# Graph layer with residual and norm on one core: constants of the compares in PSUM, picks on four banks, more chunks gathered, codes of edges by bf16 products

## The chip, the core and the metric

One core of a Trainium2 chip runs the whole layer in one launch. Its engines work side by side, each in the order of its own queue: TensorE (PE, matmuls; PEld are its weight loads), VectorE (DVE), ScalarE (ACT), GpSimd (POOL, which here issues the indirect gathers) and SyncE (SP, which issues the other transfers). They meet at semaphores. The metric is device time in microseconds, the median of three runs.

## What is computed

12,500 nodes with 128 features, 400,000 edges sorted by destination, two types of edge.

```python
Xs = X[src]
m_data = Xs @ W_data.T + b_data
m_ctrl = Xs @ W_control.T + b_control
msg = where((edge_types == 0)[:, None], m_data, m_ctrl)
agg = segment_sum(msg, dst, num_segments=N)
out = relu(agg + X @ W_self.T + b_self)
x = layernorm(x + out)
```

The kernel sums the rows of X by destination and type first and multiplies by the weights afterwards, which gives the same sums with far fewer products. A row of X is kept as three bf16 parts of 128 columns that add up to the float32 value, so a row has 384 columns.

## The kernel before

**Chunks and groups.** 128 edges are a chunk; 3125 chunks make 25 groups of 125 (`GC`). Since edges are sorted, a chunk's destinations lie in a narrow window of rows. A group has five pairs of windows: five chunks that are *gathered* (`PB`), then 20 that are *picked* (`EC`). A pair's picked part is called a set. `sets(g)` says how many sets a group has: five where `g % EACH == 0`, else four, and then the last window's 25 chunks are all gathered. With `EACH = 3` that is 109 sets and 945 gathered chunks.

**Gathered chunks.** POOL issues one indirect DMA a chunk, which fetches 128 rows of 384 bf16 from DRAM into `msg` (`fetch`, L887; 18 buffers). PE multiplies its three parts by a 0/1 matrix `psel` (L803 through `add_rows`), and DVE adds the result to the accumulator (L876). `paced` ties each gather to a matmul: there are eleven such places in a set, and a gather is due 14 chunks before its use (`AHEAD`).

**Picked chunks.** X itself lies in SBUF (`x3`). A set's 2560 edges are sorted into 98 cells by source block with 32 slots each: DVE builds one-hot matrices and running counts (`give_slots`, L541 to L713), and the result comes back by way of DRAM as `pick`, which DVE turns into 0/1 (L790). A cell's rows are then picked by PE: `pick` (128x32) times a block of `x3` (384 columns), four cells side by side in the four 32-row strips of a PSUM bank (L997). ACT casts the bank to bf16 (`emsg`, L1011), and PE multiplies by the 0/1 matrix `esel` (L803). Edges of overfull cells are fetched by a second kind of indirect DMA, `both` (L963), once for two sets.

**Turns.** A set goes in five turns of five cell rows (`bounds` 0, 5, 10, 15, 19, 24; `unit`, `rows`). A turn uses a tile of two banks and one of three (`got2`, `got3`): 5 x 4 matmuls of 384 columns. With the bank of `side` and the two of `sums` all eight banks are taken. In the fourth turn the 25th cell row is picked in halves.

**Compares.** `select` (L541) makes every one-hot matrix on DVE by comparing a constant row (`cell_col0/1`, `rank_col`, `code_col`, `near_col`, bf16 in SBUF) with codes that are repeated in pairs. A set has five: `O` (2000 columns), `rm` (640) and `esel` (1720, 1548, 1032); a window of gathered chunks has `psel` (1200, always for 25 chunks).

**Codes.** `prep(g)` turns a group's sources, destinations and types into codes: DVE subtracts the window's first row (`rel`, L498), marks the type (`kind`, L499) and adds type times width (`code`, L500 and L501); PE transposes three float32 tiles (L508); ACT writes them out.

**Order.** Work is written down set by set: `merged` sorts the pieces of a set by a position between 0 and 1, `in_turn` chains DVE's own steps in a list with such positions, and the recording layer then orders each engine's queue by its own model of times. When a group's last window is done, its sums are passed on and finished (`pass_on`, `finish`).

Of the kernel before, what the change touches and what calls it, by code (L numbers as in the profile page):

```python
# [8 lines left out]
FP = mybir.dt.float32  # L9
BF = mybir.dt.bfloat16  # L10
# [9 lines left out]
P = 128  # L20
D = 128
# [13 lines left out]
EACH = 3  # L35
# [173 lines left out]
def short_path(ctx, tc, const, ident, eps, wT, brow, bad, x, src, dst, etype, ws, bs, out):  # L209
# [10 lines left out]
    psg = ctx.enter_context(tc.tile_pool(name="psg", bufs=1, space=PSUM))  # L220

# [12 lines left out]
    def sets(g):  # L234

        return NE if g % EACH == 0 else NE - 1

# [115 lines left out]
    near_col = table(2 * PW, 0, "near_col")  # L353
    ident_b = keep.tile([P, P], BF, name="ident_b")
# [41 lines left out]
    bounds_of, from_of, pick_first = row_tables(nc, keep, tmp)  # L396
    least = tmp.tile([1, NG, NWIN], FP, name="least")
# [81 lines left out]
    def prep(g):  # L479
# [3 lines left out]
        width = bounds_of[:GC, v, 0:1]  # L483
        sf = pre.tile([GC, P], FP, name="sf", bufs=1)
        rel = pre.tile([GC, 2, P], BF, name="rel", bufs=1)
        code = pre.tile([GC, 2, P], FP, name="code_r", bufs=1)
        kind = pre.tile([GC, P], FP, name="kind_r", bufs=1)
# [7 lines left out]
        def rows():  # L495
            near = near_of(g, d)
            for k in range(2):
                nc.vector.tensor_scalar(rel[:, k], d, near[k], None, op0=OP.subtract)  # L498
            nc.vector.tensor_single_scalar(kind, t, 0.0, op=OP.not_equal)  # L499
            nc.vector.scalar_tensor_tensor(code[:, 1], kind, width, rel[:, 1], op0=OP.mult, op1=OP.add)  # L500
            nc.vector.scalar_tensor_tensor(code[:, 0], kind, float(PW), rel[:, 0], op0=OP.mult, op1=OP.add)  # L501
            for j, op in enumerate((OP.max, OP.min)):
                nc.vector.tensor_tensor(worst[:GC, v, j], worst[:GC, v, j], rel, op=op)
# [297 lines left out]
    def add_rows(out, msg, sel, start, stop):  # L801
        for j in range(3):
            last = nc.tensor.matmul(  # L803
                out, msg[:, j * D:(j + 1) * D], sel, start=(start and j == 0), stop=stop, skip_group_check=True
            )
        return last
# [116 lines left out]
    def gathered(g, i):  # L923
# [9 lines left out]
        def chunk(c):  # L933
# [9 lines left out]
            add_rows(rows, s["msg"], sel, c == 0, c == n - 1)  # L943
# [24 lines left out]
    def picked(w, tiled, ending, before):  # L968
# [26 lines left out]
        def pick(ps, q, a0=0, a1=4, last=None):  # L995
            for a in range(a0, a1):
                last = behind(last, lambda: nc.tensor.matmul(  # L997
                    ps[CAP * a:CAP * (a + 1), :], slots[w]["pick"][:, a * NQ + q, :],
                    x3[:, 4 * q + a - a0].rearrange("p j d -> p (j d)"), start=True, stop=True, skip_group_check=True,
                ))  # L1000
            return last

        def rows(q, n, room, half=False):
            ps = psg.tile([P, room, 512], FP, name=f"got{room}")
            msg = two.tile([P, room, 3 * D], BF, name=f"emsg{room}")
            for k in range(n):
                last = pick(ps[:, k, :3 * D], q + k, last=last if k else None)
                s["msg"][q + k] = msg[:, k, :]
            if half:
                last = pick(ps[:, n, :3 * D], NQ - 1, lead, lead + 2, last)  # L1010
            s["out"] = nc.scalar.copy(msg[:, :n], ps[:, :n, :3 * D])  # L1011
            if half:
                nc.scalar.copy(s["msg"][NQ - 1][half_rows, :], ps[half_rows, n, :3 * D])
            return last
# [8 lines left out]
        def unit(t):  # L1023

            if t == 3:
                assert not spare
                if "both" in slots[w]:
                    slots[w]["last"] = two.tile([P, 3 * D], BF, name="last", bufs=1)
                s["msg"][NQ - 1] = slots[w]["last"]
            paced(w + (t + 0.5) / turns, rows(bounds[t], 2, 2))  # L1030
            if t == 1 and w > 0 and w % 2 == 0:
                spare.append(lambda: spare_rows(w))
            gate = rows(bounds[t] + 2, bounds[t + 1] - bounds[t] - 2, 3, t == 3)
# [13 lines left out]
            if t == 2:  # L1047
                paced(w + (t + 1) / turns, gates[-1])
# [203 lines left out]
    for w in range(pairs):  # L1252
# [63 lines left out]
        for p in closed.pop(w, []):  # L1316
            gp, ip = divmod(p, NE)
            if ip == NE - 1:
                rest.append(lambda gp=gp: pass_on(gp))
                if gp < NG - 1:  # L1320
                    rest += finish(gp, range(4))
                if gp + 2 < NG:
                    rest.append(lambda gp=gp: begin_acc(gp + 2))
# [143 lines left out]
```

## Time and profile before

| what | us |
|---|---|
| median of three runs | 1671.41 |
| lowest, highest | 1670.22, 1672.55 |
| the profiled execution | 1674.53 |
| its span, first to last instruction | 1672.8 |

How the core's time divides over the run (busy in tenths, 40 equal slices):

```profile
PE   1699999999999999999999999999999999999988
DVE  9799998999999999999999999999999999999983
ACT  7677776777777778667777778677777777777764
POOL 1377777767787787888787887878787787888881
PEclk9899999999999999999999999999999999999999
```

A slice is 42 us. The first two are the setup, in which X is split into its three parts; from there on the sets follow each other evenly, and the last slice is the end of the last group. In the body DVE and PE are busy nearly throughout, ACT and POOL about three quarters. [...] The chain of waits, followed back from the end, runs mostly over DVE and PE:

```profile
DVE 57%; PE 25%; issue 7%; ACT 6%; DMA 3%; DVEq 2%; SPq 0%; POOL 0%; ACTq 0%; POOLq 0%
```

### The profile page before, as it was taken

Reading aid. Unit: us, or ns where it says so; the run is one execution under the profiler, and the core shown is the slowest. Engines: PE = TensorE matmul, PEld = TensorE weight load, DVE = VectorE, ACT = ScalarE, POOL = GpSimd, SP = SyncE. Lnnn points to the kernel's source line nnn. Section 1 sums busy time; section 2 is a strip of 40 time slices with the busy share of each in tenths; the row PEclk is TensorE's granted clock in tenths of the full one; section 3 lists DMA queues with packets and bytes.
Section 4 is the critical chain, followed back from the end, with each engine's and each line's share of the span. In section 5 each row is a group of like instructions: output and inputs, shape, how many; then the busy total and the mean of one; then the engine's idle time right before and its main releaser. Section 6 shows DMA issues by size and latency. Waiting matters only on the chain.

```text
span 1672.8 us, 67687 instructions
## 1 busy us (share of the span) xinstructions
PE 1542.5 (92%) x27966; PEld 1218.8 (73%) x27966; DVE 1566.8 (94%) x4078; ACT 1221.0 (73%) x2056; POOL 1244.2 (74%) x1022
## 2 busy tenths in 40 slices
PE   1699999999999999999999999999999999999988
PEld 0477777777777777777777777777777777777766
DVE  9799998999999999999999999999999999999983
ACT  7677776777777778667777778677777777777764
POOL 1377777767787787888787887878787787888881
PEclk9899999999999999999999999999999999999999
DMA  7944444554455454444454445454545444554541
GB/s 223 283 142 136 143 139 134 154 148 141 142 156 145 147 155 133 150 140 143 149 156 139 148 142 152 139 159 135 158 124 164 147 144 131 157 152 126 151 124 33
DMA packets 147605, 246.05 MB, mean 147 GB/s; under 512 B 35565, under 2 KB 114264, under 8 KB 147288
## 3 DMA queue, kind: packets, MB, share of 16 engines
q1 hardware_dynamic: 99128, 142.50, 25.4%
q0 software_dynamic: 48160, 99.14, 22.8%
q8 instruction: 221, 3.62, 0.9%
q14 instruction: 96, 0.79, 0.1%
HBM read 224.04 MB, written 17.52 MB: 144 GB/s over the span
## 4 chain that ended last, share of the span: by engine, by line
DVE 57%; PE 25%; issue 7%; ACT 6%; DMA 3%; DVEq 2%; SPq 0%; POOL 0%; ACTq 0%; POOLq 0%
PE sums L803 11%; DVE esel L541 8%; PE got L997 7%; DVE prod L656 5%; DVE prod L648 5%; DVE pick L790 5%; DVE O L541 4%; DVE rv L713 3%; DVE prod L627 3%; ACT emsg L1011 3%; PE side L1118 2%; DVE psel L541 2%; DVE found L666 2%; DVE rm L541 2%; DVE prod L612 2%
## 5 line engine op out<-in xcount | busy, mean ns | idle before, releaser
L887 POOL DMA_INDIRECT msg<-rows,idx_g x945 | 1174.7, 1243 | 302.4 <-issue 124.3
L1011 ACT CAST emsg<-got 128x768 bf16<-128x768 f32 x1090 | 964.5, 930 | 302.9 <-PE got L997 287.7
L803 PE MATMUL sums<-esel,emsg 128*128 128x172 bf16 x7848 | 693.1, 238 | 7.3 <-DVE acc L876 4.1
L803 PEld LDWEIGHTS <-emsg 128*128 128x128 bf16 x7848 | 570.8, 98 | 115.1 <-issue 104.2
L997 PE MATMUL got<-x,pick 128*32 128x384 bf16 x10682 | 561.7, 330 | 13.5 <-ACT emsg L1011 5.4
L997 PEld LDWEIGHTS <-pick 128*32 128x32 bf16 x10682 | 242.3, 96 | 140.0 <-issue 19.9
L541 DVE TENSOR_TENSOR esel<-code_col,code 128x1720 bf16<-128x1720 bf16 x327 | 292.8, 896 | 6.4 <-PE sums L803 6.3
L803 PE MATMUL sums<-psel,msg 128*128 128x48 bf16 x2835 | 162.6, 184 | 5.2 <-DVE acc L876 4.7
L803 PEld LDWEIGHTS <-msg 128*128 128x128 bf16 x2835 | 134.9, 97 | 14.1 <-issue 11.9
L656 DVE TENSOR_TENSOR prod<-prod 128x1200 bf16<-128x1200 bf16 x218 | 136.3, 625 | 5.5 <-DVE prod L648 1.2
L648 DVE TENSOR_TENSOR prod<-O,ahead 128x2000 bf16<-128x2000 bf16 x109 | 130.7, 1199 | 2.7
L541 DVE TENSOR_TENSOR O<-cell_col,blk 128x2000 bf16<-128x2000 bf16 x109 | 129.8, 1191 | 0.5 <-ACT blk L443 0.5
L963 POOL DMA_INDIRECT both<-rows,idx x55 | 64.4, 1171 | 70.0 <-DMA srcs<-in_src_dram 25.8
L726 PE MATMUL side<-rv,O 128*128 128x64 bf16 x2180 | 84.8, 195 | 32.9 <-DVE rv L713 32.0
L790 DVE TENSOR_SCALAR pick<-pick,lane_f 128x3200 bf16<-128x3200 bf16 x109 | 112.7, 1034 | 2.4 <-DMA pick<-there 2.4
L726 PEld LDWEIGHTS <-O 128*128 128x128 bf16 x2180 | 80.1, 100 | 43.0 <-DVE rv L713 24.8
L541 DVE TENSOR_TENSOR psel<-near_col,near 128x1200 bf16<-128x1200 bf16 x125 | 95.9, 767 | 0.0
L627 DVE TENSOR_TENSOR prod<-prod 128x500 bf16<-128x500 bf16 x327 | 94.3, 288 | 0.4
L713 DVE TENSOR_TENSOR rv<-rm,vals 128x1280 bf16<-128x1280 bf16 x109 | 89.4, 820 | 0.0
L622 DVE TENSOR_TENSOR prod<-O 128x1000 bf16<-128x1000 bf16 x109 | 73.9, 678 | 2.1 <-DVE bits L701 0.3
L876 DVE TENSOR_TENSOR acc<-acc,sums 128x172 f32 (+2 forms) x234 | 65.5, 280 | 6.3 <-PE sums L803 6.2
L642 DVE TENSOR_REDUCE ahead<-side 128x100 bf16<-128x200 f32 x109 | 39.2, 360 | 34.2 <-PE side L634 33.6
(197 smaller groups left out, 1522.4 us busy)
## 6 DMA issues: line engine op xcount, KB each, us to landing
pick<-there SPq DMA_DIRECT2D x108, 800.0 KB
msg<-rows,idx_g POOLq DMA_INDIRECT x945
acc<-acc_start SPq DMA_DIRECT2D x23, 640.0 KB
rows<-x SPq DMA_DIRECT2D x6, 1344.0 KB
xs<-in_x_dram SPq DMA_DIRECT2D x99, 62.5 KB
out_dram<-h SPq DMA_DIRECT2D x99, 62.5 KB
xt<-in_x_dram SPq DMA_DIRECT2D x6, 896.0 KB
cnt<-cnt_start SPq DMA_DIRECT2D x22, 160.0 KB
```

What stands on the lines that cost most here:

```text
L541: ins = nc.vector.tensor_tensor(sel.rearrange("p n (w t) -> p n w t", t=2), col[:rows].rearrange("p (o w t) -> p o w t", o=1, t=2).to_broa ...
L622: return nc.vector.tensor_add(h[:, :2 * CQ], s["O"][:, :2 * CQ], s["O"][:, 2 * CQ:])
L627: return nc.vector.tensor_add(h[:, to:to + n], h[:, a:a + n], h[:, b:b + n])
L648: return nc.vector.tensor_tensor(s["prod"][:, :, :NCELL], s["O"], s["ahead_b"].rearrange("p (o j) -> p o j", o=1).to_broadcast([P, EC, NCE ...
L656: return nc.vector.tensor_add(prod[:, :, :h], prod[:, :, :h], prod[:, :, h:2 * h])
L713: placed[:] = [nc.vector.tensor_tensor(rv.rearrange("p c v (r t) -> p c v r t", t=2), s["rm"].rearrange("p c (o r t) -> p c o r t", o=1, t ...
L726: nc.tensor.matmul(s["rk"][:m, :2 * CAP], s["held"][:, c * NCELL:c * NCELL + m], s["rv"][:, c].rearrange("p v r -> p (v r)"), start=(c == ...
L790: return nc.vector.tensor_scalar(t, t, lane_f, None, op0=OP.is_equal)
L803: last = nc.tensor.matmul(out, msg[:, j * D:(j + 1) * D], sel, start=(start and j == 0), stop=stop, skip_group_check=True)
L887: return nc.gpsimd.indirect_dma_start(out=msg, out_offset=None, in_=rows3[:, :], in_offset=bass.IndirectOffsetOnAxis(ap=codes["p", g][0][: ...
L997: last = behind(last, lambda: nc.tensor.matmul(ps[CAP * a:CAP * (a + 1), :], slots[w]["pick"][:, a * NQ + q, :], x3[:, 4 * q + a - a0].rea ...
L1011: s["out"] = nc.scalar.copy(msg[:, :n], ps[:, :n, :3 * D])
```

## The change

It has five parts.

1. *Constants in PSUM.* After the setup DVE copies `cell_col0/1`, `rank_col`, `code_col` and `near_col` into one PSUM bank (`cols`), and `select` reads them there. The codes that they are compared with stay in SBUF.
2. *Picks on four banks.* To free that bank, a turn uses two tiles of two banks (`got0`, `got1`). Four cell rows have 384 columns of a bank each; the fifth (`shared`) is split into its three parts of 128 columns, which take the last 128 columns of three banks. A turn has 4 x 4 matmuls of 384 columns and 3 x 4 of 128. `msg[j]` may now come from different tiles.
3. *`EACH` from 3 to 6.* 105 sets in place of 109; 1025 gathered chunks in place of 945.
4. *Codes.* `kind` is bf16; PE computes the code while it transposes, as `rel` times the identity plus `kind` times a scaled identity (`type_step`), in bf16. The two DVE operations on `code` go.
5. *Paths around them.* A twelfth place for gathers in a set (after the fourth turn), and a group is passed on when both its last gathered window and its last set are done (`ended`).

```diff
-EACH = 3
+EACH = 6
...
+    cols = psc.tile([P, 512], FP, name="cols")
+
+    def on_psum(t):
+        n = t.shape[1] // 2
+        at = cols[:, used[0]:used[0] + n]
+        used[0] += n
+        nc.vector.tensor_copy(at, t.bitcast(FP))
+        return at.bitcast(BF)
+
+    used = [0]
+    cell_cols = [on_psum(t) for t in cell_cols]
+    rank_col, code_col, near_col = on_psum(rank_col), on_psum(code_col), on_psum(near_col)
...
+    type_step = keep.tile([P, 3, P], BF, name="type_step")
+    for v in range(2):
+        nc.vector.tensor_scalar(type_step[:, v], ident_b, bounds_of[:, v, 0:1], None, op0=OP.mult)
+    nc.vector.tensor_scalar(type_step[:, 2], ident_b, float(PW), None, op0=OP.mult)
...
-            nc.vector.scalar_tensor_tensor(code[:, 1], kind, width, rel[:, 1], op0=OP.mult, op1=OP.add)
-            nc.vector.scalar_tensor_tensor(code[:, 0], kind, float(PW), rel[:, 0], op0=OP.mult, op1=OP.add)
...
-            for k, each in enumerate((sf, code[:, 1], code[:, 0])):
-                nc.tensor.transpose(ps[:, k * P:k * P + GC], each, ident[:GC, :GC])
+            nc.tensor.transpose(ps[:, :GC], sf, ident[:GC, :GC])
+            for k, of in ((1, v), (0, 2)):
+                turned = ps[:, (2 - k) * P:(2 - k) * P + GC]
+                for j, (each, scale) in enumerate(((rel[:, k], ident_b), (kind, type_step[:, of]))):
+                    nc.tensor.matmul(
+                        turned, each, scale[:GC, :GC], start=(j == 0), stop=(j == 1), skip_group_check=True
+                    )
...
-        def rows(q, n, room, half=False):
-            ps = psg.tile([P, room, 512], FP, name=f"got{room}")
-            msg = two.tile([P, room, 3 * D], BF, name=f"emsg{room}")
-            for k in range(n):
-                last = pick(ps[:, k, :3 * D], q + k, last=last if k else None)
-                s["msg"][q + k] = msg[:, k, :]
+        def rows(q, n, k, half=False):
+
+            ps = psg.tile([P, 2, 512], FP, name=f"got{k}")
+            msg = two.tile([P, 2, 512], BF, name=f"emsg{k}")
+            shared = NQ - 1 if half else q + 2
+            first, last = (q, None) if k == 0 else (q + n - 2, None)
+            parts = (0, 1) if k == 0 else (2,)
+            for j in range(2):
+                last = pick(ps[:, j, :3 * D], first + j, last=last)
+                s["msg"][first + j] = [msg[:, j, d * D:(d + 1) * D] for d in range(3)]
+            for j, d in enumerate(parts):
+                ends = (lead, lead + 2) if half else (0, 4)
+                last = pick(ps[:, j, 3 * D:], shared, *ends, slice(d, d + 1), last)
+                if not half:
+                    s["msg"].setdefault(shared, []).append(msg[:, j, 3 * D:])
             if half:
...
+            else:
+                width = 1024 if k == 0 else 512 + 3 * D
+                s["out"] = nc.scalar.copy(*(t.rearrange("p k d -> p (k d)")[:, :width] for t in (msg, ps)))
...
-            if t == 2:
+            if t in (1, 3):
                 paced(w + (t + 1) / turns, gates[-1])
...
+    ended = {}
+    for g in range(NG):
+        last_p = next(w for w, ps in closed.items() if g * NE + NE - 1 in ps)
+        ended.setdefault(max(last_p, each_e.index((g, sets(g) - 1))), []).append(g)
```

How the instructions stand on the engines, at three places. On PE, one turn of picks before (`got` with its number is a PSUM tile, `x_104` is `x3`; the rows left out repeat the two above them):

```order
L803 MATMUL sums<-psel,msg 128x2x24
L997 LDWEIGHTS pick
L997 MATMUL got_16496<-x_104,pick 32x384
...
L997 MATMUL got_16509<-x_104,pick 32x384
...
L747 LDWEIGHTS cell
L747 MATMUL side<-ident_b,cell 32x25
```

and one turn of the change (`x_107` is `x3`):

```order
L821 MATMUL sums<-psel,msg 128x2x24
L1015 LDWEIGHTS pick
L1015 MATMUL got_15811<-x_107,pick 32x384
...
L1015 MATMUL got_15811<-x_107,pick 32x128
...
L1015 MATMUL got_15832<-x_107,pick 32x384
...
L1015 MATMUL got_15832<-x_107,pick 32x128
...
L821 LDWEIGHTS emsg_15705
```

Behind eight of the 384-wide matmuls of the first tile now stand eight of 128 columns, and behind eight of the second four; each has a weight load of its own.

On DVE, a set's chain from `found` (the sum that ranks an edge in its cell) to `O`, the next set's one-hot matrix, before:

```order
L666 TENSOR_REDUCE found<-prod 128x20
L541 TENSOR_TENSOR psel<-near_col,near_21340 128x1200
L612 TENSOR_TENSOR prod<-blk_23906,blk_185 128x20x20
L671 CAST rank<-found 128x40
L541 TENSOR_TENSOR esel<-code_col,code 128x1720
L541 TENSOR_TENSOR rm<-rank_col,rank 128x640
L678 SCALAR_TENSOR_TENSOR key<-rank,pk 128x20
L713 TENSOR_TENSOR rv<-rm,vals_21339 128x1280
L686 MAX top<-key 128x8
L790 TENSOR_SCALAR pick<-pick,lane_f 128x3200
L541 TENSOR_TENSOR O<-cell_col_144,blk_23906 128x2000
```

and in the change (another set; `cols` are the constants in PSUM, L640 is the step called `tens`):

```order
L684 TENSOR_REDUCE found<-prod 128x20
L630 TENSOR_TENSOR prod<-blk_8546,blk_194 128x20x20
L689 CAST rank<-found 128x40
L559 TENSOR_TENSOR rm<-cols,rank 128x640
L696 SCALAR_TENSOR_TENSOR key<-rank,pk 128x20
L731 TENSOR_TENSOR rv<-rm,vals_8028 128x1280
L704 MAX top<-key 128x8
L808 TENSOR_SCALAR pick<-pick,lane_f 128x3200
L559 TENSOR_TENSOR O<-cols,blk_8546 128x2000
L559 TENSOR_TENSOR esel<-cols,code 128x1720
L640 TENSOR_TENSOR prod<-O 128x10x100
L559 TENSOR_TENSOR esel<-cols,code 128x1548
```

The 1720-wide compare, which serves the next set's first two turns, has moved from ahead of `rm` to behind `O`; the other steps keep their order.

On DVE again, a group's codes before (`rel` and `kind_r` are made ahead of these rows or between them, `worst` is a check on the range):

```order
L498 TENSOR_SCALAR rel<-dsts,near_all 125x128
L499 TENSOR_SCALAR kind_r<-typs 125x128
L503 TENSOR_TENSOR worst<-worst,rel 125x256
L500 SCALAR_TENSOR_TENSOR code_r<-kind_r,bounds_of,rel 125x128
L501 SCALAR_TENSOR_TENSOR code_r<-kind_r,rel 125x128
L503 TENSOR_TENSOR worst<-worst,rel 125x256
L642 TENSOR_REDUCE ahead<-side 128x100
```

and in the change:

```order
L513 TENSOR_SCALAR rel<-dsts,near_all 125x128
L645 TENSOR_TENSOR prod<-prod 128x100
L514 TENSOR_SCALAR kind_r<-typs 125x128
L516 TENSOR_TENSOR worst<-worst,rel 125x256 x2
L894 ISA
L894 TENSOR_TENSOR acc<-acc,sums 128x2x86
L660 TENSOR_REDUCE ahead<-side 128x100
```

The two operations on `code_r` are gone, and nothing stands in their place.

More of the change, by code (lines that the diff above doesn't have):

```diff
@@ L803, in add_rows @@
             last = nc.tensor.matmul(
-                out, msg[:, j * D:(j + 1) * D], sel, start=(start and j == 0), stop=stop, skip_group_check=True
+                out, msg[j], sel, start=(start and j == 0), stop=stop, skip_group_check=True
             )
@@ L942, in chunk @@
             rows = cells_of(s["ps"], AW, 0).rearrange("p (t w) -> p t w", t=2)[:, :, at:at + PW]
-            add_rows(rows, s["msg"], sel, c == 0, c == n - 1)
+            add_rows(rows, [s["msg"][:, j * D:(j + 1) * D] for j in range(3)], sel, c == 0, c == n - 1)
             if c == 0:
@@ L1028, in unit @@
                     slots[w]["last"] = two.tile([P, 3 * D], BF, name="last", bufs=1)
-                s["msg"][NQ - 1] = slots[w]["last"]
-            paced(w + (t + 0.5) / turns, rows(bounds[t], 2, 2))
+                s["last"] = slots[w]["last"]
+                s["msg"][NQ - 1] = [s["last"][:, d * D:(d + 1) * D] for d in range(3)]
+            n = bounds[t + 1] - bounds[t]
+            paced(w + (t + 0.5) / turns, rows(bounds[t], n, 0, t == 3))
             if t == 1 and w > 0 and w % 2 == 0:
                 spare.append(lambda: spare_rows(w))
-            gate = rows(bounds[t] + 2, bounds[t + 1] - bounds[t] - 2, 3, t == 3)
+            gate = rows(bounds[t], n, 1, t == 3)
             if t == 0:
@@ L1315, in short_path @@
         rest = []
[L1316 to L1323, printed above, removed]
+        closed.pop(w, None)
+        for gp in ended.pop(w, []):
+            rest.append(lambda gp=gp: pass_on(gp))
+            if gp < NG - 1:
+                rest += finish(gp, range(4))
+            if gp + 2 < NG:
+                rest.append(lambda gp=gp: begin_acc(gp + 2))
     ending()
```

19 lines of the change are left out of this document (9 added, 10 removed).

## The prediction

> **What bounds the kernel now.** I read the page first (busy time by engine), then busy time by windows, then the waits, then the gathers alone, then the timeline of one set.
>
> ```profile
> span 1672.8 us, 67687 instructions
> PE 1542.5 (92%) x27966; PEld 1218.8 (73%) x27966; DVE 1566.8 (94%) x4078; ACT 1221.0 (73%) x2056; POOL 1244.2 (74%) x1022
> 840.00:1008.00 168.00, 161.82 (x2982) 129.66 (x2983) 162.58 (x422) 124.01 (x212) 135.08 (x109) 1.00 0.50 152
> DVE ahead L642 <- PE side L634: 33.6, 42, 2.2
> PEld L803: 0.7, 2
> ```
>
> The third line is one window of 168 us in the middle (PE, PEld, DVE, ACT, POOL, granted clock, share of the DMA engines, GB/s): DVE is busy 162.58 of 168, PE 161.82, ACT 124. The clock is at 1.00, so no term here is one of the throttle. DVE's largest single wait is for the product before `ahead`, 33.6 us in all. The last line says who waited for gathered rows: PE's weight loads, 0.7 us in the whole run. So the gathers are early enough; DVE, with PE closely coupled to it, sets the pace. POOL looks free at 74%, but its gaps tell otherwise:
>
> ```profile
> L887 POOL DMA_INDIRECT msg<-rows,idx_g x945: 945/1122/4102, 66.8 to 1636.2; - x189
> L803 PE MATMUL sums<-psel,msg x2835: 182/183/248, 91.1 to 1658.5; 128*128 128x48 bf16 x189
> L887 POOL DMA_INDIRECT msg<-rows,idx_g x945 | 1174.7, 1243 | 302.4 <-issue 124.3 <-PE got L997 72.5 <-PE sums L803 64.0
> L963 POOL DMA_INDIRECT both<-rows,idx x55 | 64.4, 1171 | 70.0 <-DMA srcs<-in_src_dram 25.8 <-ACT emsg L1011 21.5 <-ACT idx L591 13.9
> 930.88 0.94 POOL L887 DMA_INDIRECT msg<-rows,idx_g  x1 [0.30 <-PE sums L803]
> 941.69 1.66 POOL L887 DMA_INDIRECT msg<-rows,idx_g  x1 [0.30 <-issue]
> 930.91 0.22 DVE L876 TENSOR_TENSOR acc<-acc,sums 128x80 f32 x1
> 941.34 1.19 DVE L541 TENSOR_TENSOR O<-cell_col,blk 128x2000 bf16<-128x2000 bf16 x1
> ```
>
> A gather takes 945 ns at best, 1243 in the mean, and 0.30 us lie ahead of each whatever released it. That is 945 x (1.243 + 0.30) = 1458 us, and 55 x 1.47 = 81 for the rows of overflowing cells: 1539 of the 1571 us from the first to the last gather (66.8 to 1637.4). **POOL is 98% taken.** The mean lies 298 ns above the best because of DVE: the gather at 941.69 found the compare `O` running, which ended 0.84 us later, and took 1.66 = 0.84 + 0.82; the gather at 930.88 found `acc`, which reads one operand from PSUM, and took 0.94. I read: a gather that meets a DVE operation with both operands in SBUF waits for its end; one that meets an operation with an operand in PSUM doesn't.
>
> **Four sets fewer (109 to 105).**
>
> ```profile
> 943.35 0.96 DVE L541 TENSOR_TENSOR esel<-code_col,code 128x1548 bf16<-128x1548 bf16 x1
> 946.84 0.37 DVE L642 TENSOR_REDUCE ahead<-side 128x100 bf16<-128x200 f32 x1 [1.37 <-PE side L634]
> 956.63 0.96 DVE L541 TENSOR_TENSOR esel<-code_col,code 128x1548 bf16<-128x1548 bf16 x1
> 947.70 1.00 PE L997 MATMUL got<-x,pick 128*32 128x384 bf16 x20
> 948.63 1.29 PE L803 MATMUL sums<-esel,emsg 128*128 128x172 bf16 x15
> 949.75 0.31 PE L803 MATMUL sums<-psel,msg 128*128 128x48 bf16 x6
> 950.00 1.00 PE L997 MATMUL got<-x,pick 128*32 128x384 bf16 x18
> ```
>
> From one 1548-wide compare to the next are 13.28 us, 1.37 of them idle, and no gathered window lies in between: a set costs DVE 11.9 us. Four sets: **-47.6 us**. The windows of gathered chunks stay 125, each with the same `psel` over all 25 chunks, so the 80 gathered chunks add on DVE only a wider add in four windows: +0.7 us by L876, 80 against 172 columns (below). On PE a set has 98 picks at 0.93 us for 20 (4.6 us) and 75 sums at 1.12 for 15 (5.6 us): -41 us for four; a gathered chunk costs half of 0.25 us, 80 of them +10. PE: -31 us.
>
> **Codes of edges.**
>
> ```profile
> 959.11 0.35 DVE L500 SCALAR_TENSOR_TENSOR code_r<-kind_r,bounds_of,rel 125x128 f32<-125x128 f32 x1
> 959.37 0.28 DVE L501 SCALAR_TENSOR_TENSOR code_r<-kind_r,rel 125x128 f32<-125x128 f32 x1
> 959.57 0.29 DVE L503 TENSOR_TENSOR worst<-worst,rel 125x256 bf16<-125x256 bf16 x1
> ```
>
> Start to start the two take 0.26 + 0.20 us; 25 groups: **-11.5 us** of DVE. PE gets four bf16 products for two fp32 transposes in a group: half a microsecond either way at most by the matmuls below, 25 times, on an engine that isn't the bound; I take nothing. The eight new operations of the setup (five copies, three scaled identities) cost some 0.2 us each, like L501: +1.6, wholly on the front.
>
> **Constants in PSUM.** On DVE the question is what a compare costs with its first operand there.
>
> ```profile
> L541 DVE TENSOR_TENSOR O<-cell_col,blk 128x2000 bf16<-128x2000 bf16 x109 | 129.8, 1191 | 0.5 <-ACT blk L443 0.5
> L541 DVE TENSOR_TENSOR esel<-code_col,code 128x1720 bf16<-128x1720 bf16 x109 | 113.9, 1045 | 6.0 <-PE sums L803 5.9
> L541 DVE TENSOR_TENSOR esel<-code_col,code 128x1548 bf16<-128x1548 bf16 x109 | 103.8, 953 | 0.4 <-PE sums L803 0.4
> L541 DVE TENSOR_TENSOR psel<-near_col,near 128x1200 bf16<-128x1200 bf16 x125 | 95.9, 767 | 0.0
> L541 DVE TENSOR_TENSOR esel<-code_col,code 128x1032 bf16<-128x1032 bf16 x109 | 75.0, 688 | 0.0
> L541 DVE TENSOR_TENSOR rm<-rank_col,rank 128x640 bf16<-128x640 bf16 x109 | 53.2, 488 | 2.6
> L876 DVE TENSOR_TENSOR acc<-acc,sums 128x172 f32 x109 | 35.3, 324 | 6.2 <-PE sums L803 6.2
> L876 DVE TENSOR_TENSOR acc<-acc,sums 128x80 f32 x109 | 23.9, 220 | 0.0
> ```
>
> Between 1548 and 2000 columns a compare grows by 0.527 ns a column, which leaves 137 ns fixed. `acc`, with one operand in PSUM, grows by 104/92 = 1.13 ns a (4-byte) column and leaves 130 fixed. So the fixed part shows no price for PSUM. The rate of 2-byte operands from PSUM is in no row: at best nothing changes, at worst a column costs twice as much (a rival, below). I take no change, since a pair of 2-byte elements is the one 4-byte word that `acc` reads at about this rate per word. [...]
>
> On POOL the gain is in the waits. A gather that starts at random meets an operation of length L in proportion to L and waits half of it, so each group counts by number times length squared: compares 109 x (1.19² + 1.05² + 0.95² + 0.69² + 0.49²) + 125 x 0.77² = 524.
>
> ```profile
> L648 DVE TENSOR_TENSOR prod<-O,ahead 128x2000 bf16<-128x2000 bf16 x109 | 130.7, 1199 | 2.7
> L790 DVE TENSOR_SCALAR pick<-pick,lane_f 128x3200 bf16<-128x3200 bf16 x109 | 112.7, 1034 | 2.4 <-DMA pick<-there 2.4
> L713 DVE TENSOR_TENSOR rv<-rm,vals 128x1280 bf16<-128x1280 bf16 x109 | 89.4, 820 | 0.0
> L656 DVE TENSOR_TENSOR prod<-prod 128x1200 bf16<-128x1200 bf16 x109 | 85.6, 786 | 5.5 <-DVE prod L648 1.2 <-DVE acc L876 0.7
> L622 DVE TENSOR_TENSOR prod<-O 128x1000 bf16<-128x1000 bf16 x109 | 73.9, 678 | 2.1 <-DVE bits L701 0.3 <-issue 0.3
> ```
>
> What stays in SBUF counts 109 x (1.20² + 1.03² + 0.82² + 0.79² + 0.68²) = 464, and more with the shorter ones. The compares make about half of the waiting: 0.149 of 0.298 us a gather. A gather then takes 1.094 us. **POOL after:** 1025 x 1.394 + 53 x 1.40 = 1503 us, where 1539 were. Between none (1.243, 1660 us) and all (0.945, 1350 us) I take this. With POOL never idle the span would be 66.8 + 1503 + some 17 (the 14 us that follow the last use, which starts at 1658.5, and an estimated 3 from gather to use) = 1587; with 2% idle as before, 1617.
>
> **Picks on four banks.** 20 matmuls of 384 columns in a turn become 16 of 384 and 12 of 128.
>
> ```profile
> 955.78 0.19 PE L747 MATMUL side<-ident_b,cell 128*32 128x25 bf16 x4
> 955.90 1.29 PE L803 MATMUL sums<-esel,emsg 128*128 128x172 bf16 x15
> ```
>
> Four column tiles of 384 take 0.93/5 = 0.186 us; by columns three fours of 128 make up one of them: nothing. If four short ones took the 0.12 us of these four, a turn would cost 0.17 us more and 105 x 5 turns +91. I take nothing: same line, same operands, and the columns set the time there. ACT converts the same columns in as many instructions, but one small one more a set; its 26% idle hides that.
>
> **Moved.** DVE now has `O` and often `tens` ahead of the 1720-wide compare.
>
> ```profile
> 950.17 1.05 DVE L541 TENSOR_TENSOR esel<-code_col,code 128x1720 bf16<-128x1720 bf16 x1
> 958.91 1.28 PE L803 MATMUL sums<-esel,emsg 128*128 128x172 bf16 x15
> ```
>
> Its user on PE started 7.7 us after its end here. Moved to just ahead of the 1548-wide compare that stood at 956.63, it would end some 2.3 us before its use: still in time, and a slip stops PE first. The later end of a group (pass-on and finish) moves the same instructions. SP loses four pairs of transfers; 12 places for gathers a set hold the 10.3 needed.
>
> **Sum.** DVE: 1672.8 - 47.6 - 11.5 + 1.6 + 0.7 = 1616, with its idle time kept. POOL asks 1587 to 1617, so the two meet; I add 4 us of waiting between them: span 1620. The profiled execution took 1674.53, 1.7 over its span and 3.1 over the median of the runs (1671.41), so on the scale of the median: **1619 us**, -3.1%.
>
> **Rivals.**
> - *POOL becomes the bound.* For: 98% taken, and 78 gathers net are added. Against: half its waits are met under compares. The span would be 84 + 75 + 1025 x (d + 0.30) with d the length of a gather: 1614 at 1.12, 1665 at 1.17, which is where it stops being a gain. If d falls only to there: 1640 to 1670 us.
> - *Slower: the gathers keep waiting under the compares.* The constants leave SBUF but the codes stay there; should one operand in SBUF be enough to hold a gather, d stays 1.243 and the span is 84 + 78 + 1582 = 1744 us. Against: the gather at 930.88.
> - *Slower: compares lose their pairs.* At one column where two went, the 6940 columns of a set x 105 and 150,000 of `psel` cost 0.527 ns more each: +463, 2082 us. Against: `acc` draws a 4-byte word from PSUM each 1.13 ns, and a pair of 2-byte elements is one such word in 1.05 ns, so PSUM gives what the pairs need; that DVE pairs them there is in no row, so 0.07. [...]
> - *Short picks bound PE.* +91 - 31 = +60 on PE, which has 3.7% idle by the window: up to 1672 us; I'd look for 1640.
>
> **How the numbers follow.** Forecast 0.64 (1600 to 1640), POOL bound 0.14, short picks 0.06, gathers still waiting 0.07, pairs lost 0.07, something quicker 0.02. About 0.2% can be told from no change here. Faster 0.84, same 0.02, slower 0.14. The range 1600 to 1668 holds the first three and leaves 0.16 to 0.18 out.
>
> **What would show it.** Compares with `cols` at 1191, 1045, 953 ns as before (twice that: pairs lost); no gather that ends 0.82 us after a compare; mean gather near 1.09 us; PE's loads waiting for `msg` by a few us (tens: POOL bound); fours of 128-wide picks some 60 ns apart (over 100: the PE rival). I am wrong if DVE's busy share falls below 94% in the middle windows.

## The result, and the profile after

The changed kernel takes **1640.74 us** (1638.62 to 1642.04, four runs) where the kernel before took 1670.82 on the same chip: ratio 0.982, 95% interval 0.9807 to 0.9833. The forecast was 1619. The experiments below ran on five chips; three of them run the kernel before in 1955 to 1980 us and two in 1670 to 1672, so every run is read against the kernel before on its own chip.

The page, the window in the middle, the tile `msg` and the waits, in the columns of the prediction's first rows:

```profile
span 1638.6 us, 74120 instructions
PE 1511.5 (92%) x31202; PEld 1247.9 (76%) x31202; DVE 1532.0 (93%) x3932; ACT 1201.1 (73%) x2097; POOL 1160.6 (71%) x1100
840.00:1008.00 168.00, 161.16 (x3328) 132.68 (x3327) 160.58 (x408) 123.54 (x218) 127.38 (x117) 1.00 0.51 152
L905 POOL DMA_INDIRECT msg<-rows,idx_g x1025: 940/947/2048, 66.8 to 1605.5; - x171
DVE ahead L660 <- PE side L652: 34.7, 40, 2.9
PEld L821: 0.7, 1
DVE 53%; PE 29%; issue 7%; ACT 6%; DMA 2%; DVEq 2%; SPq 0%; ACTq 0%
```

DVE still sets the pace by its busy share (160.58 of 168 us, 95.6%), and the chain of waits (last line) still runs mostly over DVE and PE. PE's 161.16 says less, since its records overlap: one of the sums with `esel` lasts 237 ns, and the next begins 74 ns after it (medians). PE's loads still wait 0.7 us for gathered rows, so POOL didn't become the bound. The groups that carried the terms of the sum:

```profile
L905 POOL DMA_INDIRECT msg<-rows,idx_g x1025 | 1094.3, 1068 | 353.6 <-issue 140.5 <-PE got L1015 89.3 <-PE sums L821 87.0
L981 POOL DMA_INDIRECT both<-rows,idx x53 | 61.2, 1154 | 67.5 <-DVE rm L559 25.4 <-ACT emsg L1043 20.6 <-ACT idx L609 9.7
L559 DVE TENSOR_TENSOR O<-cols,blk 128x2000 bf16<-128x2000 bf16 x105 | 125.0, 1190 | 0.5 <-ACT blk L460 0.5
L559 DVE TENSOR_TENSOR esel<-cols,code 128x1720 bf16<-128x1720 bf16 x105 | 109.0, 1038 | 0.9 <-PE sums L821 0.9
L559 DVE TENSOR_TENSOR esel<-cols,code 128x1548 bf16<-128x1548 bf16 x105 | 99.8, 950 | 0.0
```

The compares cost on DVE what they cost before (1190, 1038, 950 ns against 1191, 1045, 953). A gather now takes 1068 ns in the mean, 121 above the best, where 298 were; POOL has 1025 x 1.368 + 53 x 1.454 = 1479 us of work. Before, 368 of the 667 gathers of over 1 us ended within 0.025 us of 0.82 us behind the end of a compare; after, of 270 such gathers none does. What fell short is DVE: its busy time went down by 34.8 us (1566.8 to 1532.0), where the sum of the prediction had -56.8.

Where DVE's time went can be read from start to start. Each operation is followed by the next after some shortest spacing for its shape (the fourth percentile over the traces); what lies above it I sorted by what stands there. A step depends on the one ahead of it where it has to wait for it, because it reads its result or overwrites what it read. From 66 us to the last DVE operation, in us (number of intervals), with the last experiment beside it:

| DVE from start to start | before | after | `three_moved` |
|---|---|---|---|
| operations at their shortest spacing | 1431.8 | 1380.6 | 1383.0 |
| gap behind a step that the next one depends on | 48.2 (557) | 63.1 (677) | 23.8 (304) |
| gap elsewhere, under 0.26 each | 35.0 | 34.9 | 30.2 |
| `rank` casts that last over 0.22 | 0.1 (1) | 8.8 (58) | 0.9 (7) |
| around the load of a window's place | 11.2 | 13.1 | 72.3 |
| longer waits | 69.5 | 60.6 | 118.4 |
| sum | 1595.9 | 1561.0 | 1628.6 |

The work fell by 51.2 us. The prediction's -58.4 (sets, codes, wider add) held about 6 of gaps and waits (4/109 of 164 us), so 52.4 were due: that part is right. But the gaps behind dependent steps rose by 14.9 us and the stretched casts by 8.7, together 23.6. Both are seen in two sets of the timeline of DVE and POOL (start, us, operation, in brackets the idle time ahead):

```profile
929.77 0.30 DVE L679 TENSOR_TENSOR prod<-prod 128x280 bf16<-128x280 bf16 x1
930.11 0.48 DVE L684 TENSOR_REDUCE found<-prod 128x20 f32<-128x320 bf16 x1
930.63 0.38 DVE L630 TENSOR_TENSOR prod<-blk,blk 128x400 bf16<-128x400 bf16 x1
930.92 0.34 DVE L689 CAST rank<-found 128x40 bf16<-128x40 f32 x1
931.29 0.49 DVE L559 TENSOR_TENSOR rm<-cols,rank 128x640 bf16<-128x640 bf16 x1
944.59 0.18 DVE L689 CAST rank<-found 128x40 bf16<-128x40 f32 x1
944.68 0.26 DVE L894 TENSOR_TENSOR cnt<-cnt,sums 64x120 f32 x1
...
930.30 0.94 POOL L981 DMA_INDIRECT both<-rows,idx  x1 [0.30 <-ACT emsg L1043]
```

`found` depends on the step at 929.77, which is called `eighth`, and starts 0.34 us after it. The same step takes 0.21 us to the next start where an independent operation follows, as in `three_moved` (the last experiment below):

```profile
940.99 0.29 DVE L679 TENSOR_TENSOR prod<-prod 128x280 bf16<-128x280 bf16 x1
941.20 1.04 DVE L559 TENSOR_TENSOR esel<-cols,code 128x1720 bf16<-128x1720 bf16 x1
```

The cast at 930.92 began 0.62 us into a gather, ended with it (931.26 against 931.24) and took 0.34 instead of 0.18 us. All the casts before and after (ns min/median/max):

```profile
L671 DVE CAST rank<-found x109: 168/177/326, 26.8 to 1617.7; 128x40 bf16<-128x40 f32 x109
L689 DVE CAST rank<-found x105: 166/273/415, 26.1 to 1588.5; 128x40 bf16<-128x40 f32 x105
```

All 58 long casts end 4 to 14 ns behind the end of a gather. Not every cast that meets a gather is held: 90 began inside one, and the 32 that began less than 0.13 or more than 0.43 us ahead of its end took their usual time. Before, 74 began inside a gather, but only one of them between 0.22 and 0.43 us ahead of its end, and that one was held.

### The profile page after: what moved, and what is told of

Same layout as the page of the kernel before. It is cut to its first block, busy times and chain, and to the rows that moved or that the text cites. A ratio compares the mean times of both kernels' runs of the same rounds, so it can differ in the third digit from the quotient of the medians.

```text
span 1638.6 us, 74120 instructions
## 1 busy us (share of the span) xinstructions
PE 1511.5 (92%) x31202; PEld 1247.9 (76%) x31202; DVE 1532.0 (93%) x3932; ACT 1201.1 (73%) x2097; POOL 1160.6 (71%) x1100
## 4 chain that ended last, share of the span: by engine, by line
DVE 53%; PE 29%; issue 7%; ACT 6%; DMA 2%; DVEq 2%; SPq 0%; ACTq 0%
PE sums L821 12%; PE got L1015 9%; DVE esel L559 7%; DVE prod L674 5%; DVE prod L666 5%; DVE O L559 4%; DVE pick L808 4%; PE side L1150 4%; DVE prod L645 3%; DVE rv L731 3%; DVE prod L640 3%; DVE rm L559 2%; DVE found L684 2%; DVE psel L559 2%; DVEq L877 2%
## 5 line engine op out<-in xcount | busy, mean ns | idle before, releaser
L905 POOL DMA_INDIRECT msg<-rows,idx_g x1025 | 1094.3, 1068 | 353.6 <-issue 140.5
L1043 ACT CAST emsg<-got 128x1024 bf16<-128x1024 f32 x840 | 771.1, 961 | 184.0 <-PE got L1015 166.4
L1015 PE MATMUL got<-x,pick 128*32 128x384 bf16 (+1 forms) x14070 | 552.5, 286 | 10.1 <-ACT last L1040 3.5
L559 DVE TENSOR_TENSOR esel<-cols,code 128x1720 bf16<-128x1720 bf16 (+2 forms) x315 | 280.7, 892 | 1.3 <-PE sums L821 0.9
L1038 ACT CAST emsg<-got 128x768 bf16<-128x768 f32 x210 | 168.3, 802 | 122.9 <-PE got L1015 116.4
L559 DVE TENSOR_TENSOR O<-cols,blk 128x2000 bf16<-128x2000 bf16 x105 | 125.0, 1190 | 0.5 <-ACT blk L460 0.5
L744 PE MATMUL side<-rv,O 128*128 128x64 bf16 (+1 forms) x2100 | 81.9, 195 | 23.5 <-DVE rv L731 23.1
L744 PEld LDWEIGHTS <-O 128*128 128x128 bf16 (+1 forms) x2100 | 76.5, 100 | 26.3 <-DVE rv L731 23.4
L559 DVE TENSOR_TENSOR psel<-cols,near 128x1200 bf16<-128x1200 bf16 x125 | 96.0, 768 | 0.3 <-issue 0.3
L645 DVE TENSOR_TENSOR prod<-prod 128x500 bf16<-128x500 bf16 (+2 forms) x315 | 90.0, 286 | 0.6
L640 DVE TENSOR_TENSOR prod<-O 128x1000 bf16<-128x1000 bf16 x105 | 71.1, 677 | 1.2
L660 DVE TENSOR_REDUCE ahead<-side 128x100 bf16<-128x200 f32 x105 | 37.6, 358 | 35.6 <-PE side L652 34.7
```

The source lines that it names most:

```text
L559: ins = nc.vector.tensor_tensor(sel.rearrange("p n (w t) -> p n w t", t=2), col[:rows].rearrange("p (o w t) -> p o w t", o=1, t=2).to_broa ...
L645: return nc.vector.tensor_add(h[:, to:to + n], h[:, a:a + n], h[:, b:b + n])
L744: nc.tensor.matmul(s["rk"][:m, :2 * CAP], s["held"][:, c * NCELL:c * NCELL + m], s["rv"][:, c].rearrange("p v r -> p (v r)"), start=(c == ...
L905: return nc.gpsimd.indirect_dma_start(out=msg, out_offset=None, in_=rows3[:, :], in_offset=bass.IndirectOffsetOnAxis(ap=codes["p", g][0][: ...
L1015: last = behind(last, lambda: nc.tensor.matmul(out[CAP * a:CAP * (a + 1), :], slots[w]["pick"][:, a * NQ + q, :], x3[:, 4 * q + a - a0, pa ...
L1038: s["out"] = nc.scalar.copy(msg[:, :, :3 * D], ps[:, :, :3 * D])
```

## The experiments

Theories: **A**, the shortfall is order on DVE: the 1720-wide compare no longer stands between steps that depend on each other, and each such pair costs some 0.12 us more. **D**, a cast that meets a gather at the wrong moment waits for its end. **B**, gathers or POOL set the pace. **C**, PE does.

**1. The compare back into the chain; `found` in PSUM; constants in SBUF.** Four kernels on one chip, where the kernel before took 1980.41 us.

`early_found` and `early_rm` (the second at position 0.545) put the compare into the list of DVE's steps; the set that uses it takes it from `first_sel`:

```diff
+    def choose_first(w, prev):
+        sel = sp.tile([P, 10, 2 * EW], BF, name="esel", bufs=3)
+        first_sel[w], ins = select(sel, code_col, slots[w]["code"][:, 0:10], prev)
+        return ins
...
+            (0.515, (lambda prev: choose_first(w + 1, prev)) if w + 1 < pairs and chain else None),
```

`found_psum`, and `const_sbuf`:

```diff
-            s["found"] = two.tile([P, EC], FP, name="found")
+            at = 400 + EC * (w % 2)
+            s["found"] = cols[:, at:at + EC]
```

```diff
-    cell_cols = [on_psum(t) for t in cell_cols]
-    rank_col, code_col, near_col = on_psum(rank_col), on_psum(code_col), on_psum(near_col)
```

> The changed kernel with one thing moved: the next set's 1720-wide compare stands on DVE between eighth and found (103 of 105 sets) instead of behind O or among tens and the folds. Theory A (the shortfall is order on DVE: two steps that depend on each other cost 0.12 us more when they follow directly, 0.339 against 0.215 us start to start for eighth to found): 90 such gaps close, -11 us; some 50 places where the compare stood between dependent folds open, up to +6: 1630 to 1636 us, eighth at 0.22 us start to start. Theory B (gathers or POOL set the pace) and theory C (PE with its short and interrupted picks sets the pace): DVE's order is off the path, 1638 to 1644 us.

> The same compare put between rank and rm (101 of 105 sets). Theory A: the gap rank to rm closes instead (0.12 us x 94 = -11 us), the one from eighth to found stays at 0.339 us, up to +6 where the compare stood before: 1630 to 1636 us. The rank casts that last 0.33 us instead of 0.18 (58 of 105) stay, since the compare comes behind them. Theories B and C: 1638 to 1644 us.

> The changed kernel with the 20 sums of found written to PSUM, in the bank of the constants, so that the rank cast reads PSUM. Theory D (the cast with both operands in SBUF waits for the end of a gather that it meets, 8.9 us in all over 58 casts): all casts last about 0.18 us, the time falls by about 9 us to 1630 to 1634 us. If the long casts have another cause (the operation in front of them, an ACT or PE wait): casts stay at 0.33 us in half of the sets, 1638 to 1644 us.

> The changed kernel with the five constants left in SBUF (picks on four banks, 105 sets, codes by PE as in the change). Theory (the constants in PSUM carry the change by freeing the gathers): gathers wait for compares again, mean 1.20 to 1.25 us, POOL 1025 x 1.54 + 53 x 1.47 = 1657 us plus 84 in front and behind: 1700 to 1745 us, PE's loads wait for msg by tens of us. Rival (four sets fewer and the picks carry it, gathers lead their use far enough anyway): 1635 to 1660 us, PE waits under 5 us for msg.

Measured: 2051.54, 2049.70, 2045.31 and 2048.93 us, ratios 1.0353, 1.0335, 1.0322 and 1.0331 (intervals about 0.003 either way). All four alike, and all slower than before: on this chip none of the edits shows in the time. (The changed kernel itself didn't run there.) The waits of PE's weight loads, first in `early_found`, then in the changed kernel on its chip:

```profile
PEld L1022 <- issue: 277.0, 578, 2.0
PEld L821 <- issue: 131.7, 410, 1.3
```

```profile
PEld L821 <- issue: 81.1, 316, 1.5
PEld L1015 <- issue: 18.1, 65, 1.1
```

Ahead of the picks PE pauses 277 us with nothing that the profile shows to wait for, where it paused 18, and the chain of waits of `early_found` runs over PE for 67% of the span. That fits theory C here: the kernels with 31,202 matmuls lose to the one with 27,966, though no run there changes the picks alone. So the times decide nothing between A, B and D. What the traces show: with `found` in PSUM the casts keep one length, and with the constants in SBUF the gathers wait again (`found_psum`, then `const_sbuf`):

```profile
L690 DVE CAST rank<-cols x105: 181/192/195, 26.2 to 1987.6; 128x40 bf16<-128x40 f32 x105
L906 POOL DMA_INDIRECT msg<-rows,idx_g x1025 | 1048.6, 1023 | 763.1 <-PE got L1016 297.3 <-PE sums L822 285.9 <-issue 112.3
```

```profile
L687 DVE CAST rank<-found x105: 166/178/396, 27.1 to 1992.8; 128x40 bf16<-128x40 f32 x105
L903 POOL DMA_INDIRECT msg<-rows,idx_g x1025 | 1193.3, 1164 | 647.2 <-PE sums L819 227.5 <-PE got L1013 215.0 <-issue 123.3
```

Between these two the mean gather differs by 141 ns, and by 130 from the means of `early_found` and `early_rm` (1033 and 1034); the forecast had 149. The order on DVE differs between them too. In `const_sbuf` PE's loads wait 0.5 us for gathered rows, as the rival to the constants said, but where PE pauses that says little. D fits (no cast over 195 ns in `found_psum`, where `const_sbuf` reaches 396), but long casts were rare on this chip (14 to 24 of 105 in the runs with `found` in SBUF). `const_sbuf` shows one thing more: with the constants in SBUF the 1720-wide compare is back between `eighth` and `found` (52 sets) or `found` and `same`, the step behind it (24). So it is the move to PSUM that moved it, by way of the order that the recording layer chose.

**2. The same edits again, and both together,** on two more chips (before: 1954.83 for the first two, 1975.78 for the third). `early4` and `both_moves` have a fourth buffer for `esel`; `both_moves` joins them with `found` in PSUM.

```diff
-        sel = sp.tile([P, 10, 2 * EW], BF, name="esel", bufs=3)
+        sel = sp.tile([P, 10, 2 * EW], BF, name="esel", bufs=4)
```

> The changed kernel with the next set's 1720-wide compare between eighth and found (103 of 105 sets) and a fourth buffer for esel, so that the compare waits for no sums there. Where PE's instructions come without pauses (a run of 28 picks at 0.93 us): theory A (directly following dependent steps) 1626 to 1636 us, ratio 0.973 to 0.979, eighth at 0.22 us start to start; theories B (gathers) and C (PE) 1638 to 1644 us, ratio 0.981 to 0.984. Where PE pauses between its instructions (the kernel before at 1980 us): no statement on A, ratio 1.03.

> The sums of found in PSUM, otherwise the changed kernel. Where PE's instructions come without pauses: theory D (the cast with both operands in SBUF waits for the end of a gather that it meets) all 105 casts at 0.18 to 0.20 us, 1630 to 1634 us, ratio 0.975 to 0.978; without D 1638 to 1644 us, ratio 0.981 to 0.984, and half the casts at 0.33 us.

> The changed kernel with both: the next set's 1720-wide compare between eighth and found (fourth buffer for esel) and the sums of found in PSUM. Where PE's instructions come without pauses (the kernel before at about 1671 us): theories A and D together (dependent steps directly behind each other; casts that wait for the end of a gather) 1616 to 1628 us, ratio 0.967 to 0.974, eighth at 0.22 us start to start, all casts under 0.20 us; theories B (gathers) and C (PE): 1637 to 1644 us, ratio 0.980 to 0.984. Where PE pauses between its instructions (the kernel before at 1950 us or more): ratio 1.03 as in the runs before this one, since DVE's time is not on the path there.

Measured: 2018.14, 2020.17 and 2058.37 us, ratios 1.0327, 1.0326 and 1.0401. PE pauses there too (ahead of the picks 267 us in `early4`, 269 and 280 in the others), so the times are inconclusive on A and D. In the traces both effects are as expected: `eighth` is followed after 0.22 us in `early4` (median), and the casts with `found` in PSUM take 182 to 200 ns. The pauses don't fall at random: of the 578 in `early_found`, 290 stand ahead of the same load of PE's queue as one in `early4` on another chip, where chance would give 23.

**3. DVE made the bound by hand, and PE made light.** On a chip with the kernel before at 1670.43 us.

The heavy pair has `both_moves`' buffers and `found`, and around the product `rv`:

```diff
+            for _ in range(9):
```

with the compare at 0.59 in `heavy_none`, and in `heavy_three`, against that:

```diff
-            (0.59, (lambda prev: choose_first(w + 1, prev)) if w + 1 < pairs and chain else None),
+            (0.515, (lambda prev: choose_first(w + 1, prev)) if w + 1 < pairs and chain else None),
-            (0.6, (lambda prev: pick_matrix(w + 1, prev)) if w + 1 < pairs else None),
+            (0.545, (lambda prev: pick_matrix(w + 1, prev)) if w + 1 < pairs else None),
-            (0.62, started("blocks")),
+            (0.525, started("blocks")),
```

The light pair, in `add_rows` (`const_light` has the edit of `const_sbuf` as well):

```diff
-        for j in range(3):
+        for j in range(1):
```

> The changed kernel made heavy on DVE, so that DVE and not PE bounds it also where PE pauses between its instructions: the product rv is computed nine times over instead of once (8 x 0.82 us x 105 sets = +689 us, 128 x 1280 elements, the same result each time). found lies in PSUM, esel has a fourth buffer, and the 1720-wide compare stands between rv and the pick compare, where it fills no gap: 745 DVE steps follow directly behind the step they depend on. Expected 2260 to 2340 us, DVE busy over 93%. It is the base of the next run.

> As the run before, with three independent operations moved into the chain: the 1720-wide compare between eighth and found, O of a later set between found and same, the pick compare between rank and rm. 397 direct dependent steps instead of 745, no operation added or removed. Theory A (a dependent step that follows directly starts 0.12 us later): 348 x 0.12 = 42 us less than the run before, at least 30. Rival (the gaps are taken up by waits for PE or gathers elsewhere, so order on DVE doesn't set the time): within 6 us of the run before.

Measured: 2418.12 and 2404.51 us, ratios 1.4485 (1.4455 to 1.4514) and 1.4385 (1.4360 to 1.4411): 13.6 us less, between theory and rival. (Both lie above what was expected of the first; the granted clock had fallen to 0.84 and 0.85.) By the sorting above, the gaps that A counts fell from 64.9 to 26.7 us, 38 as A says; but the time around the load of a window's place rose from 13.0 to 45.7. That load stands in DVE's own queue behind `O`, and I had moved `O` away from ahead of it. The pair has a second flaw: `found` lies in the bank from which the compares read, and two compares now stand next to it. From the 1720-wide compare to `found` pass 1.08 us (67 sets), and from `found` to `O` 0.53 (80 sets), where `three_moved`, with `found` in SBUF, has 0.96 and 0.39. The trace names the one ahead as what was waited for in nearly all of them, so some 18 us of new gaps opened. The pair is no clean test of A.

> The changed kernel made light on PE: of the three bf16 parts of each row only the first is multiplied in the sums of gathered and picked chunks (the two lower parts are left out of the result; 7090 matmuls fewer, about 424 us of PE by 74 and 25 ns each). Expected, DVE bound: 1560 to 1640 us, mean gather 1.03 to 1.10 us, POOL 1025 x 1.37 + 53 x 1.46 = 1483 us. It is the base of the next run.

> As the run before (the lower parts left out too), with the five constants of the compares left in SBUF. Theory (the constants in PSUM carry the change, since without them gathers wait for compares and POOL becomes the bound): mean gather 1.20 to 1.26 us, PE's loads wait for msg by tens of us, 1680 to 1745 us. Rival (gathers lead their use far enough, DVE stays the bound): within 1% of the run before, PE's loads wait under 5 us for msg.

Measured: 1855.29 and 1891.20 us, ratios 1.1111 (1.1089 to 1.1134) and 1.1328 (1.1301 to 1.1354). The base missed by over 200 us: with less to do PE became slower. Windows of `after_light` (us, PE, PEld, DVE, ACT, POOL busy, then the granted clock), two of its matmuls with the idle time ahead of them, and a wait:

```profile
840.00:848.00 8.00, 4.84 (x95) 3.32 (x92) 5.86 (x13) 5.60 (x8) 6.16 (x6) 0.96 0.65 192
848.00:856.00 8.00, 4.78 (x64) 3.34 (x64) 4.97 (x16) 0.73 (x2) 2.23 (x3) 0.50 0.19 54
856.00:864.00 8.00, 5.41 (x94) 3.25 (x82) 3.98 (x13) 5.10 (x12) 4.99 (x6) 0.71 0.57 173
847.48 0.22 PE L821 MATMUL sums<-psel,msg 128*128 128x48 bf16 x1 [2.21 <-DMA msg<-rows,idx_g]
849.08 0.53 PE L821 MATMUL sums<-psel,msg 128*128 128x48 bf16 x2 [1.37 <-DMA msg<-rows,idx_g]
PEld L1015 <- issue: 211.3, 662, 1.4
```

PE idles for 2.2 us up to 847.48 and for 1.4 up to 849.08, and from 848 to 856 the granted clock is 0.50; over the run it is 0.887 (0.994 in the changed kernel). The low clock stands beside the idle time here; that the one causes the other no run shows. Nor is the clock all that differs. The last row has the pauses ahead of the picks, 211 us where the changed kernel had 18, on a chip that runs the kernel before in 1670 us. So the pauses aren't a matter of the chip alone; what share of the loss is theirs, and what share the clock's, isn't shown. Against that base the constants in SBUF cost 36 us more, and the waits for gathered rows show how, in `after_light` and in `const_light`:

```profile
PEld L821 <- DMA msg<-rows,idx_g: 155.0, 134, 3.5
```

```profile
PEld L819 <- DMA msg<-rows,idx_g: 240.0, 234, 3.3
L903 POOL DMA_INDIRECT msg<-rows,idx_g x1025 | 1215.4, 1186 | 491.1 <-PE got L1013 211.3 <-issue 192.6 <-PE sums L819 58.1
```

The direction is the theory's: longer gathers (1186 against 1054 ns) make PE wait for `msg`. The size in the full kernel isn't measured. By the prediction's formula and the mean of `const_sbuf` it would be 84 + 1025 x 1.464 + 78 = 1663 us, an estimate.

**4. Three operations moved, nothing added,** on a chip with the kernel before at 1671.97 us.

The three lines of `heavy_three` and its fourth buffer, without the ninefold product and with `found` in SBUF, and one line more:

```diff
-            (0.63, (lambda prev: load_place(prev, w + 1, 1)) if w + 1 < pairs else None),
+            (0.69, (lambda prev: load_place(prev, w + 1, 1)) if w + 1 < pairs else None),
```

> The changed kernel with its full work and nothing added, three operations moved into the chain on DVE: the 1720-wide compare between eighth and found, O of a later set between found and same, the pick compare between rank and rm; the load of a window's place comes after the folds, esel has a fourth buffer, found stays in SBUF. 403 direct dependent steps instead of 775. Where PE's instructions come without pauses (the kernel before at about 1671 us): theory A, 372 x 0.12 = 45 us if all of it shows, two thirds of it (as the heavy pair showed 13.6 of 20.6) 30 us: 1595 to 1615 us, ratio 0.955 to 0.967; if POOL were the next bound, not below 1587. Rival (order on DVE doesn't set the time there): 1637 to 1644 us, ratio 0.980 to 0.984. Where PE pauses (the kernel before at 1950 us or more): ratio 1.03 and no statement on A.

Measured: **1706.47 us**, ratio 1.0210 (1.0185 to 1.0234): slower than both kernels, and neither theory's number. Its column in the table has the answer. The gaps fell by 39.3 us where A had 45, and the casts, which A doesn't count, by 7.9. But the load of a place, which I had moved behind the folds (the steps that add up `tens`), lost its cover there: +59.2 us. Its three steps on DVE's queue in the changed kernel (ns min/median/max):

```profile
L877 DVEq TENSOR_LOAD <-place_i x229: 297/304/1778, 60.2 to 1600.6; - x115
L877 DVEq FUSED_REGOPS  x229: 183/190/206, 61.5 to 1601.0; - x115
L877 DVEq SEQ_ASSERT  x229: 23/23/35, 61.7 to 1601.2; - x115
```

Half a microsecond and more, hidden while `O` or another long operation runs ahead of it (1.19 us for `O`), and bare behind a fold of 0.20. And three operations of 3.3 us now stand ahead of `rv`, for which `put` waits, PE's products of `rv` with `O` (L744). What PE waited for ahead of `put` (us, times), in the changed kernel and in `three_moved`:

```profile
  DVE rv L731: 46.5, 4
  issue: 1.5, 7
```

```profile
  DVE rv L731: 98.0, 73
  issue: 57.6, 121
```

PE comes late to the sums, and DVE waits for PE in turn: `ahead` by 53.2 us instead of 34.7, and longer waits rise by 57.8 in all. A is right about the gaps and wrong that closing them in this way is worth anything.

## Why the prediction was right, and where it fell short

- *What bounds the kernel.* Right as far as the traces show: DVE, with PE closely coupled to it, before and after.
- *Four sets fewer, codes.* Right: -51.2 us of work where 52.4 were due.
- *Constants in PSUM.* On DVE right: no price for PSUM in the fixed part, and pairs kept. 1548 and 2000 columns took 950 and 1190 ns (953 and 1191 from SBUF), which is 0.53 ns a column in both and 128 ns fixed where 137 were, and an independent operation behind `O` started 1.11 us after it (median) in both. On POOL right in mechanism and size: 1068 ns a gather where 1094 was forecast, 1479 us where 1503; no gather waits for a compare, and with the constants back in SBUF the mean is 130 to 141 ns longer. What this saves in the full kernel isn't shown: the work on DVE alone fell by more than the time.
- *Picks on four banks.* Right on this chip: a full turn of picks takes 935 ns from start to start (median) where it took 929. On the chips where PE pauses, the kernels with these picks lose 3 to 4% (63 to 83 us). That is near the size of the rival of short picks (+60), but no run there keeps the old picks and the rest of the change, so that it is the rival is not shown.
- ***Moved* is the step that failed.** It said that the compare behind `O` is "still in time, and a slip stops PE first", and cost it at nothing. In time it was: no product or load of PE's sums waits for an `esel` in the trace. What it had done where it stood was forgotten: it filled gaps between dependent steps. It had not mostly stood ahead of `rm`, as the set shown before the prediction suggests (7 sets of 109), but between `eighth` and `found` (43), ahead of `eighth` (26) or behind `found` (23). And `psel`, of which nothing was said, had moved too: it stood between `eighth` and `found` in 20 more sets, and in none after. Now `found` follows directly behind `eighth` in 92 sets of 105, where it did in 33 of 109. Gaps: +14.9 us, about half of them at this place.
- *A wait that no step had:* the prediction let gathers wait for DVE, and not DVE for gathers. The `rank` cast now starts in the stretch where a gather holds it in 58 sets, where it did in 1: +8.7 us. Why it falls there so much oftener isn't shown; the gathers run at other times now, and the steps ahead of the cast too. Longer waits fell by 8.9 and the load's rose by 1.9.

The result lies 22 us above the forecast, and gaps and casts on DVE rose by 23.6, for which the forecast had nothing but 4 us of coupling. That is shown by sorting two traces; no run undid it alone on a chip where DVE is the bound. Open: whether the gaps can be filled for a gain with the load left behind `O` and `rv` no later; what the casts alone are worth; what the constants in PSUM are worth beside four sets fewer; and why PE pauses, on three chips and in the light kernels on a fourth. No version ran that beats the changed kernel.

## What to carry to other kernels

Before an operation is moved off a chain, ask what it covered there: the gap between two dependent steps on its own engine, a register load in the queue, a transfer. When a change frees one engine of waiting for another, look for the same contention the other way round. And a change that adds small matmuls should be timed on more than one chip: the changed kernel gained 2% on one, and kernels that differ from it in a step or two lost 3 to 4% on three others, where PE pauses between instructions.

## What the runs showed of the hardware

- A cast with both operands in SBUF that began 0.24 to 0.40 us ahead of a gather's end lasted until that end (58 of 105 in the changed kernel, up to 415 ns instead of 176); with its source in PSUM it took 181 to 195 ns in all 105 (`found_psum`). So DVE waits for gathers here too, the direction that I had left out, but casts that began more than 0.43 us ahead of a gather's end weren't held.
- A DVE step that depends on the one just ahead of it started about 0.12 us later in the changed kernel than an independent one did (0.34 against 0.22 us behind `eighth`, 0.52 against 0.40 behind `found`, 0.50 against 0.38 ahead of `eighth`; medians), and nothing in the busy or idle times tells it.
- With 7300 matmuls fewer (31,202 to 23,902) the kernel took 215 us longer than the changed kernel on its own chip, at a granted clock of 0.887 and with 211 us of pauses ahead of the picks.
